# A linear-attention and Mamba kernel: two rows scanned by one instruction across neighbouring PSUM banks

## The chip, the cores and the metric

The kernel runs on one core of a Trainium2 chip. The time is the device time in microseconds of one execution; of three runs of the kernel before, the median is 8722.74 us (8712.8 to 8732.38 us). A core has five engines with instruction queues of their own: PE (TensorE, matrix products), DVE (VectorE), ACT (ScalarE), POOL (GpSimd) and SP (SyncE, which here issues the transfers). They run side by side and meet only at semaphores. PSUM is the small memory that PE writes its products to; DVE and ACT can read and write it too[...]. It has eight banks of 512 fp32 values in each of the 128 partitions.

## The reference, cut to what matters

The input x is (8, 512, 48, 48): 8 samples, 512 channels, 2304 places. Two layers follow, each behind a group norm and with a residual around it. The first is causal linear attention with eight heads. The second splits the channels into four groups of 128; each group, one after the other, goes through a Mamba block, and its fused output is added to the next group's input. The heart of a Mamba block is a recurrence over the places, for 256 channels times 16 states:

```python
q = einsum('nchw,oc->nohw', gn(x), Wq); k, v = ...        # layer 0
out = x + num(q, k, v) / den(q, k)
...
delta = softplus(dt @ Wdt.T + bdt)                         # layer 1, a Mamba block
A = -exp(A_log)
dA = exp(einsum('bld,dn->bldn', delta, A))
dBu = einsum('bld,bln->bldn', delta * xs, Bm)
def step(h, inp):
    dA_t, dBu_t, C_t = inp
    h = dA_t * h + dBu_t
    return (h, einsum('bdn,bn->bd', h, C_t))
_, ys = scan(step, h0, (dA, dBu, Cm))
y = (ys + xs * D) * silu(z)
out = y @ Wo.T
```

## The kernel before, in words

**Tiling.** The 2304 places are cut into six chunks of LC = 384. A job is one chunk of one Mamba block: 8 samples x 4 blocks x 6 chunks are 192 jobs. The 256 x 16 recurrences of a job fill 128 partitions 32 times. They are worked off in eight slots of four rows, a row being one recurrence on 128 partitions over the 384 places; a slot's index is k, and 192 x 8 = 1536 slots follow one another. Two streams of jobs (even and odd samples) take turns.

**A slot.** A tile `u` of [128, 2, 2, 1 + 384] holds the four rows. Column 0 of each row is the state at the end of the chunk before. `last_product` (L849) copies it there on ACT (L855), unless the job is the first chunk of its block (`self.c` is 0), and has POOL write the last 128 columns of delta * xs * B (L856); `product` (L864) has DVE write the other 256 (L867). `decay` (L873) has ACT write exp(delta * A) of one row into one PSUM bank (L877). `scan` (L885) has DVE run the recurrence of one row in place in `u` with the decays of that bank (L888). Column 0 of the decay is exp(0), so that the scan's first step, with initial value 0, takes over the state as it stands; the zeros for it are kept in column 0 of `drs` (L120). In a first chunk the scan is 384 long and column 0 is left out. `weigh` (L898) then has POOL multiply the whole of `u` by C (L900), `keep` (L907) has ACT save the last column as the state (L911), and `gather` (L913) has PE sum the rows into the tile `yp` (L916), which has a PSUM bank of its own.

**The banks.** Six PSUM banks, six separate tiles `bank0` to `bank5` (L126), are shared by everything else: the decays; the conv, gate and small projections of the Mamba blocks (`prepare`, L681); their output projection (L934); and the whole attention (`chunk`, L273) with its products on PE, its evictions on ACT and DVE, and one ACT instruction that works in place in a bank (the Relu at L306). `take` hands out a free bank, the list `spare` holds the free ones, and `Banks` is what the tasks use to take and free them.

**The order.** The schedule is the order in which the Python code emits instructions; each engine's queue has its instructions in that order. The framework adds the waits: an instruction that writes a tile waits until the earlier reads and writes of that tile by other engines are done, and one that reads a tile waits for the earlier writes of it.

`slot(k)` (L1137) emits one slot: the product of slot k+1, the tasks that are due (`beside`), the four scans with `ahead(DEPTH)` after each, and in the middle the rest of the tasks and the POOL product of slot k+2. `ahead(n)` (L1103) emits decays until n of them stand ready and unscanned; with DEPTH = 3 ACT is up to three rows ahead of DVE. A task is a Python generator that yields when it wants to go on and how many free banks it needs; `fits` (L987) holds it back while there are fewer.

Of the kernel before, what the change touches and what calls it, by code (L numbers as in the profile page):

```python
# [9 lines left out]
F32 = mybir.dt.float32  # L10
BF16 = mybir.dt.bfloat16
AF = mybir.ActivationFunctionType
ALU = mybir.AluOpType
# [4 lines left out]
P = 128  # L18
T = 128
LC = 384  # L20
NG = 2
SLOTS = 8
TAIL = 128
BANKS = 6
DEPTH = 3
LEAD = 11
ALONE = 4

# [22 lines left out]
def attention_then_mamba_kernel(  # L51
# [17 lines left out]
    nc = tc.nc  # L69
# [5 lines left out]
    cpool = ctx.enter_context(tc.tile_pool(name="consts", bufs=1))  # L75
# [5 lines left out]
    ps1 = ctx.enter_context(tc.tile_pool(name="ps1", bufs=1, space=PSUM))  # L81
# [35 lines left out]
    for t in dbcs:  # L117
        nc.gpsimd.memset(t[32:64, :], 1.0)

    drs = [cpool.tile([P, 2, 1 + LC], F32, name=f"dr_{i}") for i in range(2)]  # L120
    for t in drs:
        nc.gpsimd.memset(t[:, :, 0:1], 0.0)

    spare = [ps1.tile([P, 512], F32, name=f"bank{i}") for i in range(BANKS)]  # L126
    hot = []

    def take(decay=False):
        first = [b for b in spare if (b.name in hot) == decay]  # L130
        b = (first or spare)[0]
        spare.remove(b)
        if b.name in hot:
            hot.remove(b.name)
        return b

    class Banks:
# [4 lines left out]

        def __call__(self):
            self.held.append(take())
            return self.held[-1]

        def free(self, n=1, late=False):
            for _ in range(n):
                b = self.held.pop(0)
                if late:  # L150
                    hot.append(b.name)
                spare.append(b)


# [9 lines left out]
    def flush(every=True):  # L164
        while stores and (every or stores[0][0] <= half_no[0] - 2):
            _, o, i = stores.pop(0)
            nc.sync.dma_start(out=o, in_=i)
# [506 lines left out]
    class Job:  # L674
# [6 lines left out]
        def prepare(self):  # L681

            st, c = self.stream, self.c
            n = self.n = f"{st.n}_{c}"
# [3 lines left out]
            bank = Banks()  # L688
# [28 lines left out]
            first = 2 * self.start  # L717
# [9 lines left out]
            ]  # L727
            ahead(DEPTH + 2)
            nc.scalar.activation(xs[:, 0, :], xc0, AF.Silu, bias=pv[:, 0:1])  # L729
# [31 lines left out]
            delta = mpool.tile([P, 2, LC], F32, tag="delta", name=f"delta_{n}", bufs=1)  # L761
            ahead(DEPTH + 2)
            for h in range(2):
# [7 lines left out]
            def spread(what):  # L771
                s = dpool.tile([256, LC], F32, tag="dscr", name=f"{what}_{n}", bufs=6)
                nc.sync.dma_start(out=s.rearrange("(h p) l -> p h l", h=2), in_=delta)
                return s.rearrange("(h g d) l -> h d g l", h=2, g=2)

            dsrc = spread("dscr")
# [5 lines left out]
            def pairs(t, rows):  # L782
                for i in range(2):
                    nc.sync.dma_start(out=t[i * 64 : i * 64 + 64], in_=rows)

            def steps(h):
                self.dr[h] = drs[h]
                pairs(self.dr[h][:, :, 1 : 1 + LC], dsrc[h])

            def scaled(h):  # L790
                self.dxr[h] = mpool.tile([P, 2, LC], F32, tag="dxr", name=f"dxr_{n}_{h}")
# [57 lines left out]
        def last_product(self, s):  # L849

            shape, cols = [P, NG, 2, TAIL], slice(LC - TAIL, LC)
            u = mpool.tile([P, NG, 2, 1 + LC], F32, tag="u", name=f"u_{self.n}_{s}", bufs=5)
            if self.c:
                h, q = s // 4, s % 4 * NG
                nc.scalar.copy(u[:, :, :, 0], self.state[:, h, q : q + NG, :])  # L855
            nc.gpsimd.tensor_tensor(  # L856
                u[:, :, :, 1 + LC - TAIL :],
                self.B[s % 4][:, :, cols].unsqueeze(2).to_broadcast(shape),
                self.dxr[s // 4][:, :, cols].unsqueeze(1).to_broadcast(shape),
                ALU.mult,  # L860
            )
            return u
# [7 lines left out]
                self.dxp.unsqueeze(1).to_broadcast(shape),  # L870
            )

        def decay(self, s, i):  # L873
            h, q, j, g = s // 4, s % 4 * NG, i // 2, i % 2
            dA = take(decay=True)
            cols = slice(0 if self.c else 1, 1 + LC)
            nc.scalar.activation(  # L877
                dA[:, cols],
                self.dr[h][:, g, cols],
                AF.Exp,  # L880
                scale=self.w[6][:, 2 * h + g, q + j : q + j + 1],
            )
            return dA

        def scan(self, s, i, u, dA):  # L885
            j, g = i // 2, i % 2
            cols = slice(0 if self.c else 1, 1 + LC)
            nc.vector.tensor_tensor_scan(  # L888
                u[:, j, g, cols],
                dA[:, cols],  # L890
                u[:, j, g, cols],
                0.0,
                ALU.mult,
                ALU.add,
            )
            spare.append(dA)

        def weigh(self, s, u):  # L898

# [74 lines left out]
    slots = SLOTS * len(jobs)  # L974
# [31 lines left out]
    tasks, heads = [], []  # L1006
# [13 lines left out]
    def finale(job):  # L1020
        yield "0", 1
        job.project()
        yield "1", 0
        job.maximum()
        if job.c == NC - 1:
            yield from job.stream.pass_on()
# [4 lines left out]
    for b in counted:  # L1031
        first = times[parts.index((b, 0, 0))]
# [19 lines left out]
    def prune():  # L1052
        tasks[:] = [t for t in tasks if t.need is not None]
        heads[:] = [t for t in heads if t.need is not None]

    def beside(half):

        half_no[0] = half
        flush(every=False)
        begin(half // 2 + LEAD)  # L1060

        for t in heads:
            if t.need is not None and t.need[1] == 0 and t.fits() and t.due():
                t.step()
        held = False
        for t in tasks + heads:
            while t.need is not None and t.due():
                if not t.fits() or held and t.need[1]:
                    held = held or t.need[1] > len(spare)
                    break  # L1070
                t.step()
        prune()
# [19 lines left out]
    def at(k):  # L1092
        return jobs[k // SLOTS], k % SLOTS

    def apart(k):

        return k % SLOTS == 0 and k > 0 and at(k)[0].c == 0 and at(k)[0].stream is at(k - 1)[0].stream

    us, decays, waiting, kept = {}, [], [], []
    todo = 0  # L1100
    primed, drawn = set(), set()

    def ahead(n):  # L1103

        nonlocal todo
        while len(decays) < n and spare and todo < 4 * slots:
            k = todo // 4
            if apart(k) and k not in primed:
                break
            job, s = at(k)  # L1110
            if not job.prepared or s // 4 not in job.dr:
                break
            decays.append(job.decay(s, todo % 4))
            todo += 1

    def close(k):

# [9 lines left out]
    def prime(k):  # L1127
# [6 lines left out]
        job.product(s, us[k])  # L1134
        ahead(DEPTH)

    def slot(k):  # L1137
        job, s = at(k)
        end = k + 1 == slots or apart(k + 1)
        if not end and k + 1 not in drawn:  # L1140
            j, r = at(k + 1)
            j.product(r, us[k + 1])
        before = jobs[k // SLOTS - 1] if k >= SLOTS else None
        if s == 2 and before is not None and not before.closed:
            before.gated(1)
            tasks.insert(0, Task(finale(before)))
        elif s == 6:
            job.gated(0)
        beside(2 * k)
        for i in range(4):  # L1150
            job.scan(s, i, us[k], decays.pop(0))
            if i == 0 and s in (2, 6):
                job.skip(s // 4)
            ahead(DEPTH)
            if i == 1:

                while kept:
                    kept.pop(0)()
                if len(waiting) > 1:
                    waiting.pop(0)()  # L1160
                if s == 2:
                    job.inputs(1)
                elif s == 6 and k + 2 < slots and not apart(k + 2):
                    j = at(k + 2)[0]
                    if not j.prepared:
                        hurry(k + 2, lambda: j.prepared)
                    j.inputs(0)
                if not end and k + 2 < slots and not apart(k + 2):
                    j, r = at(k + 2)
                    us[k + 2] = j.last_product(r)  # L1170
                    if s == 7:

                        j.product(r, us[k + 2])
                        drawn.add(k + 2)
                beside(2 * k + 1)
        u = us[k]
        job.weigh(s, u)
        kept.append(lambda: at(k)[0].keep(s, u))
        waiting.append(lambda: at(k)[0].gather(s, us.pop(k)))
        if end:  # L1180
            close(k)
            if k + 1 < slots:
                prime(k + 1)
            else:
                hurry(slots, lambda: not tasks)
                flush()
# [82 lines left out]
```

## Time and profile before

| What | us |
|---|---|
| median of 3 runs | 8722.74 |
| the profiled execution | 8723.09 |
| its span, first to last instruction | 8721.0 |
| DVE busy | 8072.2 |
| POOL busy | 7834.3 |
| PE busy | 7774.7 |
| ACT busy | 6852.0 |
| of DVE: the scans (L888), 6144 of them | 5455.4 |
| of ACT: the decays (L877), 6144 of them | 3405.1 |
| of PE: the gathering into `yp` (L916) | 2417.7 |

The span divided by the 1536 slots is 5.68 us a slot. Busy time is the time in which an engine had an instruction running; four engines are busy for 79 to 93 per cent of the span, so most of the work lies side by side. In the profile's lists of instructions "x2" behind a name stands for two of them in a row, merged into one line, and the time ahead of the engine's name is that from the first one's start to the last one's end. The granted TensorE clock (PEclk, 1 is full speed) was 0.964 on average.

### The profile page before, as it was taken

Reading aid. Unit: us, or ns where it says so; the run is one execution under the profiler, and the core shown is the slowest. Engines: PE = TensorE matmul, PEld = TensorE weight load, DVE = VectorE, ACT = ScalarE, POOL = GpSimd, SP = SyncE. Lnnn points to the kernel's source line nnn. Section 1 sums busy time; section 2 is a strip of 40 time slices with the busy share of each in tenths; the row PEclk is TensorE's granted clock in tenths of the full one; section 3 lists DMA queues with packets and bytes.
Section 4 is the critical chain, followed back from the end, with each engine's and each line's share of the span. In section 5 each row is a group of like instructions: output and inputs, shape, how many; then the busy total and the mean of one; then the engine's idle time right before and its main releaser. Section 6 shows DMA issues by size and latency. Waiting matters only on the chain. (4 is left out here: it accounts for less than half of the span.)

```text
span 8721.0 us, 124881 instructions
## 1 busy us (share of the span) xinstructions
PE 7774.7 (89%) x36482; PEld 3714.5 (43%) x36482; DVE 8072.2 (93%) x11078; ACT 6852.0 (79%) x14500; POOL 7834.3 (90%) x4343
## 2 busy tenths in 40 slices
PE   7899999988899999998889999999889999999965
PEld 4444444444444444444444444444444444444422
DVE  2899999999899999998899999999889999999998
ACT  2788888777788888877778888887777888888876
POOL 1789999999999999998998999998999889999998
PEclk9999999999999999999999999999999999999987
DMA  5667777776766777776676777776666667766665
GB/s 183 168 178 190 196 198 197 191 191 189 195 188 190 193 200 199 197 189 191 187 193 186 193 190 197 196 197 187 188 185 194 188 188 190 189 188 185 183 165 146
DMA packets 1002924, 1643.11 MB, mean 188 GB/s; under 512 B 138592, under 2 KB 797312, under 8 KB 1002240
## 3 DMA queue, kind: packets, MB, share of 16 engines
q1 hardware_dynamic: 1002240, 1635.13, 69.1%
q8 instruction: 290, 4.75, 0.2%
q14 instruction: 394, 3.23, 0.1%
HBM read 1309.06 MB, written 325.58 MB: 187 GB/s over the span
## 5 line engine op out<-in xcount | busy, mean ns | idle before, releaser
L888 DVE TENSOR_TENSOR_SCAN u<-bank,u 128x385 f32<-128x385 f32 (+1 forms) x6144 | 5455.4, 938 | 327.4 <-ACT bank L877 288.3
L900 POOL TENSOR_TENSOR u<-u,C 128x1536 f32<-128x1536 f32 x1536 | 4892.7, 3185 | 345.6 <-DVE u L888 186.9
L877 ACT ACTIVATE bank<-dr,av 128x385 f32<-128x385 f32 (+1 forms) x6144 | 3405.1, 578 | 671.0 <-DVE u L888 575.2
L916 PE MATMUL yp<-u,cst 128*64 128x384 f32 x12288 | 2417.7, 515 | 343.9 <-POOL u L900 259.6
L856 POOL TENSOR_TENSOR u<-B,dxr 128x512 f32<-128x512 f32 x1536 | 1969.9, 1283 | 17.5 <-DMA dxr<-xscr 15.4
L867 DVE TENSOR_TENSOR u<-B,dxp 128x1024 f32<-128x1024 f32 x1536 | 1835.0, 1195 | 9.7 <-ACT dxp L840 9.7
L293 PE MATMUL bank<-xn,wq_sb 128*128 128x384 f32 x4608 | 1725.8, 519 | 74.2 <-DVE u L888 33.0
L916 PEld LDWEIGHTS yp<-u,cst 128*64 128x64 f32 x12288 | 780.7, 139 | 1557.9 <-issue 871.9
L693 PE MATMUL bank<-xi,wk 128*128 128x384 f32 x3072 | 1110.7, 505 | 198.6 <-ACT kl L390 108.7
L293 PEld LDWEIGHTS bank<-xn,wq_sb 128*128 128x128 f32 x4608 | 867.4, 199 | 842.4 <-DVE u L888 140.0
L693 PEld LDWEIGHTS bank<-xi,wk 128*128 128x128 f32 x3072 | 558.8, 192 | 761.4 <-ACT kl L390 211.6
L805 POOL TENSOR_TENSOR delta<-delta,xs 128x384 f32<-128x384 f32 x384 | 385.7, 1005 | 361.8 <-DMA dscr<-delta 234.6
L305 ACT ACTIVATE ex<-bank,bqkv_sb 128x384 f32<-128x384 f32 x384 | 221.5, 577 | 505.3 <-PE bank L293 505.3
L877 ACT ACT_TABLE_LOAD x382 | 490.1, 1283 | 6.8
L845 ACT ACTIVATE yp<-xs,pv 128x384 f32<-128x384 f32 x384 | 223.6, 582 | 278.0 <-DVE yz L928 277.5
L934 PE MATMUL bank<-yz,wo 128*128 128x384 f32 x768 | 302.1, 510 | 24.4 <-DVE yz L928 17.3
L753 PE MATMUL bank<-dbc,wd 9*128 9x384 f32 x768 | 312.4, 527 | 3.7 <-ACT dbc L745 3.7
L704 PE MATMUL bank<-xi,wi 128*128 128x384 f32 x768 | 287.5, 495 | 9.7 <-ACT xs L729 9.7
L423 PE MATMUL bank<-cst,rdb 128*128 128x128 f32 x576 | 110.0, 304 | 200.9 <-DVE u L888 198.7
L740 PE MATMUL bank<-xs,wx 128*40 128x384 f32 x768 | 280.0, 487 | 2.7 <-ACT sm L457 2.7
L476 PE MATMUL bank<-sm,v 128*64 128x128 f32 x2304 | 257.1, 302 | 0.0
L729 ACT ACT_TABLE_LOAD x192 | 246.3, 1283 | 3.6 <-PE bank L693 0.2
(117 smaller groups left out, 7978.0 us busy)
## 6 DMA issues: line engine op xcount, KB each, us to landing
B<-scr SPq DMA_DIRECT2D x1536, 192.0 KB
C<-scr SPq DMA_DIRECT2D x1536, 192.0 KB
xn<-xn SPq DMA_DIRECT2D x192, 768.0 KB
dr<-dscr SPq DMA_DIRECT2D x768, 192.0 KB
dxr<-xscr SPq DMA_DIRECT2D x768, 192.0 KB
dscr<-delta SPq DMA_DIRECT2D x192, 384.0 KB
xscr<-delta SPq DMA_DIRECT2D x192, 384.0 KB
xn<-in_x SPq DMA_DIRECT2D x48, 768.0 KB
```

What stands on the lines that cost most here:

```text
L293: nc.tensor.matmul(ps, wq_sb[:, kt, j * 512 + o * P : j * 512 + (o + 1) * P], xn[:, kt, :], start=(kt == 0), stop=(kt == 3),)
L693: nc.tensor.matmul(xc, wk[:, k, h * P : (h + 1) * P], xi[:, c0 + k : c0 + k + LC], start=(k == 0), stop=(k == 3),)
L704: nc.tensor.matmul(zp, wi[:, 256 + h * P : 256 + (h + 1) * P], xi[:, c0 + 3 : c0 + 3 + LC], start=True, stop=True,)
L753: nc.tensor.matmul(vp, wd[32:41, h * P : (h + 1) * P], dbc[32:41, :], start=True, stop=True)
L805: nc.gpsimd.tensor_tensor(delta[:, h, :], delta[:, h, :], xs[:, h, :], ALU.mult)
L856: nc.gpsimd.tensor_tensor(u[:, :, :, 1 + LC - TAIL :], self.B[s % 4][:, :, cols].unsqueeze(2).to_broadcast(shape), self.dxr[s // 4][:, :, ...
L867: nc.vector.tensor_mul(u[:, :, :, 1 : 1 + LC - TAIL], self.B[s % 4][:, :, cols].unsqueeze(2).to_broadcast(shape), self.dxp.unsqueeze(1).to ...
L877: nc.scalar.activation(dA[:, cols], self.dr[h][:, g, cols], AF.Exp, scale=self.w[6][:, 2 * h + g, q + j : q + j + 1],)
L888: nc.vector.tensor_tensor_scan(u[:, j, g, cols], dA[:, cols], u[:, j, g, cols], 0.0, ALU.mult, ALU.add,)
L900: nc.gpsimd.tensor_tensor(u[:, :, :, 0:LC], u[:, :, :, 1:], self.C[s % 4].unsqueeze(2).to_broadcast([P, NG, 2, LC]), ALU.mult,)
L916: nc.tensor.matmul(self.yp[g * 64 : g * 64 + 64, 0:LC], pair_sum, u[:, j, g, 0:LC], start=False, stop=(s % 4 == 3 and j == NG - 1), skip_g ...
L934: nc.tensor.matmul(self.xm[:, 0:LC], self.w[2][:, h, :], self.yz[:, h, :], start=(h == 0), stop=(h == 1),)
```

## The change

The six bank tiles become one tile, `banks`, of 6 x 512 columns, and a bank is now a number. In an even bank the decays of a row lie in the last 384 columns, in an odd one in columns 1 to 384, and the column in front of them is set to zero once, at the start (`front`). So the decays of two rows in an even bank and the odd one behind it, each with a zero ahead, are one stretch of 2 x 385 columns. Two neighbouring rows of `u`, each with its state in column 0, are a stretch of 2 x 385 as well, and one scan instruction runs over both: at the second row's column 0 the decay is 0, so that what came before is dropped and the state is taken over.

`take_two` looks for two such free banks, `decay` writes one row or two, and `scan` takes what `decay` left. `ahead` asks for two banks when the row isn't a slot's last one, and falls back on a single row only when fewer than SINGLE = 2 rows stand ready. Column 0 of `u` is now always written: with the state, or with the zeros of `rest` in a first chunk. `take` prefers a bank whose loss leaves the most couples whole. `room` emits decays ahead of the tasks if the due tasks' banks are left over. All other users of the banks get the 384 columns that their bank's decays have.

```diff
+SINGLE = 2
...
-    drs = [cpool.tile([P, 2, 1 + LC], F32, name=f"dr_{i}") for i in range(2)]
-    for t in drs:
-        nc.gpsimd.memset(t[:, :, 0:1], 0.0)
-    spare = [ps1.tile([P, 512], F32, name=f"bank{i}") for i in range(BANKS)]
-    hot = []
+    drs = [cpool.tile([P, 2, LC], F32, name=f"dr_{i}") for i in range(2)]
+    rest = cpool.tile([P, NG, 2], F32, name="rest")
+    nc.gpsimd.memset(rest, 0.0)
+    banks = ps1.tile([P, BANKS * 512], F32, name="banks")
+    spare, hot = list(range(BANKS)), []
+
+    def front(b):
+        return 512 * b + (511 - LC if b % 2 == 0 else 0)
+
+    for b in spare:
+        nc.vector.memset(banks[:, front(b) : front(b) + 1], 0.0)
...
+    def take_two():
+        twos = [b for b in spare if b % 2 == 0 and b + 1 in spare]
+        if not twos:
+            return None
+        def rank(b):
+            return -(b in hot) - (b + 1 in hot), max(spare.index(b), spare.index(b + 1))
+        b = min(twos, key=rank)
+        drop(b)
+        drop(b + 1)
         return b
...
         def __call__(self):
             self.held.append(take())
-            return self.held[-1]
+            first = 1 + front(self.held[-1])
+            return banks[:, first : first + LC]
...
-            if self.c:
-                h, q = s // 4, s % 4 * NG
-                nc.scalar.copy(u[:, :, :, 0], self.state[:, h, q : q + NG, :])
+            h, q = s // 4, s % 4 * NG
+            nc.scalar.copy(u[:, :, :, 0], self.state[:, h, q : q + NG, :] if self.c else rest)
...
-        def decay(self, s, i):
-            ...
+        def decay(self, s, i, first, n):
+            h, q = s // 4, s % 4 * NG
+            for r in range(n):
+                j, g = (i + r) // 2, (i + r) % 2
+                nc.scalar.activation(
+                    banks[:, 1 + front(first + r) : 1 + front(first + r) + LC],
+                    self.dr[h][:, g, :],
+                    AF.Exp,
+                    scale=self.w[6][:, 2 * h + g, q + j : q + j + 1],
+                )
+            return first, n
+
+        def scan(self, i, u, entry):
+            first, n = entry
+            size, at = n * (1 + LC), front(first)
+            rows = u.rearrange("p j g l -> p (j g l)")[:, i * (1 + LC) : i * (1 + LC) + size]
+            nc.vector.tensor_tensor_scan(
+                rows, banks[:, at : at + size], rows, 0.0, ALU.mult, ALU.add
             )
-            spare.append(dA)
+            spare.extend(range(first, first + n))
+            return n
...
     def ahead(n):
-        while len(decays) < n and spare and todo < 4 * slots:
-            k = todo // 4
+        while sum(e[1] for e in decays) < n and spare and todo < 4 * slots:
+            k, i = todo // 4, todo % 4
...
-            decays.append(job.decay(s, todo % 4))
-            todo += 1
+            first = take_two() if i < 3 else None
+            if first is None and sum(e[1] for e in decays) >= SINGLE:
+                break
+            two = first is not None
+            decays.append(job.decay(s, i, first if two else take(decay=True), 1 + two))
+            todo += 1 + two
+
+    def room():
+        need = sum(t.need[1] for t in tasks + heads if t.need is not None and t.due())
+        if len(spare) >= need + 2:
+            ahead(DEPTH)
...
+        room()
         beside(2 * k)
-        for i in range(4):
-            job.scan(s, i, us[k], decays.pop(0))
-            if i == 0 and s in (2, 6):
+        ahead(DEPTH)
+        i = 0
+        while i < 4:
+            was, i = i, i + job.scan(i, us[k], decays.pop(0))
+            if was == 0 and s in (2, 6):
                 job.skip(s // 4)
-            ahead(DEPTH)
-            if i == 1:
+            if was < 2 <= i:
...
+                room()
                 beside(2 * k + 1)
+            ahead(DEPTH)
```

More of the change, by code (lines that the diff above doesn't have):

```diff
@@ L118, in attention_then_mamba_kernel, with couples, drop @@
         nc.gpsimd.memset(t[32:64, :], 1.0)
-    drs = [cpool.tile([P, 2, 1 + LC], F32, name=f"dr_{i}") for i in range(2)]
-    for t in drs:
-        nc.gpsimd.memset(t[:, :, 0:1], 0.0)
-    spare = [ps1.tile([P, 512], F32, name=f"bank{i}") for i in range(BANKS)]
-    hot = []
-    def take(decay=False):
[L130 to L134, printed above, removed]
+    drs = [cpool.tile([P, 2, LC], F32, name=f"dr_{i}") for i in range(2)]
[7 more added lines that the diff above has]
+        nc.vector.memset(banks[:, front(b) : front(b) + 1], 0.0)
+    def couples(free):
+        return sum(b + 1 in free for b in free if b % 2 == 0)
+    def drop(b):
+        spare.remove(b)
+        if b in hot:
+            hot.remove(b)
+    def take(decay=False):
+        left = {b: couples([f for f in spare if f != b]) for b in spare}
+        b = min(spare, key=lambda b: ((b in hot) != decay, -left[b], spare.index(b)))
+        drop(b)
+        return b
+    def take_two():
[5 more added lines that the diff above has]
+        b = min(twos, key=rank)
+        drop(b)
+        drop(b + 1)
         return b
@@ L150, in free @@
                 if late:
-                    hot.append(b.name)
+                    hot.append(b)
                 spare.append(b)
@@ L787, in steps @@
                 self.dr[h] = drs[h]
-                pairs(self.dr[h][:, :, 1 : 1 + LC], dsrc[h])
+                pairs(self.dr[h], dsrc[h])
             def scaled(h):
@@ L871, in product @@
             )
-        def decay(self, s, i):
[L874 to L881, printed above, removed]
-            )
[L883 to L895, printed above, removed]
-            spare.append(dA)
+        def decay(self, s, i, first, n):
[15 more added lines that the diff above has]
+                rows, banks[:, at : at + size], rows, 0.0, ALU.mult, ALU.add
+            )
+            spare.extend(range(first, first + n))
+            return n
         def weigh(self, s, u):
```

## The prediction

> **What bounds the kernel now.** I read the busy shares first, then the costliest groups, the list of waits, and last the timeline, to see what lies beside what.
>
> ```profile
> PE 7774.7 (89%) x36482; PEld 3714.5 (43%) x36482; DVE 8072.2 (93%) x11078; ACT 6852.0 (79%) x14500; POOL 7834.3 (90%) x4343
> ...
> L888 DVE TENSOR_TENSOR_SCAN u<-bank,u 128x385 f32<-128x385 f32 (+1 forms) x6144 | 5455.4, 938 | 327.4 <-ACT bank L877 288.3
> L900 POOL TENSOR_TENSOR u<-u,C 128x1536 f32<-128x1536 f32 x1536 | 4892.7, 3185 | 345.6 <-DVE u L888 186.9
> L877 ACT ACTIVATE bank<-dr,av 128x385 f32<-128x385 f32 (+1 forms) x6144 | 3405.1, 578 | 671.0 <-DVE u L888 575.2
> ...
> L293 PE MATMUL bank<-xn,wq_sb 128*128 128x384 f32 x4608 | 1725.8, 519 | 74.2 <-DVE u L888 33.0
> ```
>
> Four engines are nearly full, DVE most of all, and two thirds of DVE is the scans. DVE is idle for 8721 - 8072 = 649 us, 288 of them because a decay is late:
>
> ```profile
> DVE u L888 <- ACT bank L877: 288.3, 213, 4.5
> ```
>
> That is 213 waits in 6144 scans: ACT is otherwise ahead. The time holds only because the users of the banks work at once, as the timeline shows (start, duration, engine, line):
>
> ```profile
> 4001.19 2.85 PE L293 MATMUL bank<-xn,wq_sb 128*128 128x384 f32 x8
> ...
> 4003.02 3.50 DVE L888 TENSOR_TENSOR_SCAN u<-bank,u 128x385 f32<-128x385 f32 x4
> ...
> 4003.34 0.85 ACT L457 ACTIVATE sm<-bank 128x384 f32<-128x384 f32 x2
> ...
> 4004.08 1.08 ACT L877 ACTIVATE bank<-dr,av 128x385 f32<-128x385 f32 x2
> ...
> 4005.41 0.91 PE L462 MATMUL bank<-xr,cst 128*128 128x384 f32 x2
> ```
>
> While DVE scans from 4003.02 to 4006.52, ACT writes two decays (4004.08) and PE a product (4005.41), each to another bank. The reader should keep these 3.5 us in mind. The last view is the end of the run, where PE has less to do:
>
> ```profile
> 8580.00:8700.00 120.00, 72.55 (x231) 24.67 (x232) 108.55 (x127) 75.51 (x165) 116.13 (x64) 0.70 0.49 134
> ```
>
> ```profile
> 8606.51 5.40 PE L693 MATMUL bank<-xi,wk 128*128 128x384 f32 x8 [1.27 <-POOL xi L667]
> ...
> 8613.27 2.85 PE L693 MATMUL bank<-xi,wk 128*128 128x384 f32 x8
> ```
>
> With PE busy for 72.55 of 120 us the granted clock was 0.70, and the same eight matmuls took 5.40 us once and 2.85 us 7 us later.
>
> **What the Trainium skill says.** (1) "VectorE: DVE Perf Modes", section "The DRAIN you can't avoid": each DVE operation empties its pipeline at the end, so the count of operations is to be kept small. The trace agrees: a scan alone is 0.938 us, but four in a row take 3.50, so (3.50 - 0.938) / 3 = 0.854 us apart. (2) "PSUM — Partial Sum Buffer", section "PSUM bank collisions raise a hardware error": two engines must be kept apart on one bank and quadrant, while accesses to different banks run clean. The overlap at 4003 to 4006 us agrees; the hardware doesn't ask for an order between banks. (3) "TensorE: Matmul & The Clock Gate", part 1: after an idle window of about 3.4 us PE's clock is halved until it has been busy for about as long. 5.40 against 2.85 us agrees.
>
> **The change part by part.**
>
> *Fewer scans.* In the changed program as built there are 3071 double scans and 2 single ones, so nearly every pair is joined. A double scan isn't in the trace. Below: the two forms of 385 and 384 elements last 939 and 937 ns, so 2 ns an element, 0.938 + 0.77 = 1.71 us. Above: 0.938 + 0.854 = 1.79, nothing saved. I take 1.74. In a row, two single scans cost 1.71 of DVE's time; a double one would save at most the 0.854 - 0.77 = 0.08 us between them, 3071 x 0.08 = 250 us. That is the whole of the gain there is. 256 more copies of a zero state (193 ns each on ACT, 49 us) and one column less in each decay (1 ns) are nothing beside it, covered by ACT's 21% idle time.
>
> *One tile in place of six.* This decides. The waits are laid tile by tile, and `banks` is now one tile. I read the built program's waits: a scan of banks 2 and 3 waits for the projection matmul that was emitted just ahead of it and writes bank 0, and for the decays of the next pair in banks 4 and 5; that matmul waits for the decays before it, and a decay waits for the scan and the matmuls before it, whatever bank they used. Followed through all waits, every write to `banks` comes after every earlier access to it by another engine, and every read after every earlier write, without exception. In the program of before, of 19,666 cases of a bank write and the latest earlier one of another engine, 17,700 had no order between them. Only reads can still lie beside reads.
>
> So the accesses to `banks` form a single file: 10,766 stretches, 2328 of PE writes, 3455 of ACT writes (3071 times a pair of decays, 384 times the Relu) and 4982 of reads (3071 with a scan), one single stretch of zeros aside. Between two scans there is now always a pair of decays, and on average 2328 / 3071 = 0.76 PE stretches. The file's length is a sum, with the durations of the page:
>
> - Scans: 3071 x 1.74 = 5345 us.
> - Pairs of decays: two take 1.09 us in the timeline, overlapping; the second now waits for the first, so 2 x 0.578 + 0.04 (the gap between L406 and L407, a wait on its own engine) = 1.20. 3071 x 1.20 = 3685. Lower bound 1.09: 3347.
> - PE's writes to banks: PE's busy time less the gathering into `yp`, which comes in 1536 lines of x8 with 1.51 us, 2319 us: 7775 - 2319 = 5456 at the clock of before.
> - The Relu in place, L306: 208.8 us, say 209.
> - DVE's evictions (L350, L358, L379, L428, L945: 520; L406, L407, L413, L415: 176), some tails overlapping: 650.
> - ACT's evictions: in 1911 stretches of reads there is no scan, and 2616 of the 3024 evictions stand in these. By line (L305 221, L457 160, L364, L729, L732 112 each, L733, L734 94, L390, L391 184, parts of L486, L745, L375, L764: 240) 1330, less the overlaps of neighbours: 1250.
> - Handing over: scan to decay 0.05 us (scan ending at 4001.13, PE starting 4001.18), PE to ACT 0.03 to 0.04. 10,766 x 0.05 = 540; bounds 0.04 to 0.08, 430 to 860.
> - What stands in the queue between two steps of the file: two table loads of 1.28 us around each Softplus that a scan of 1.74 hides in part, the state copies of 0.19 us ahead of an eviction. I put 400; none at best, 900 at worst.
> - Start and end without scans: 60.
>
> The sum is 17.6 ms with PE at its old clock. The products (L867, 1.195 us) stay hidden: each stands between two scans, where DVE waits 1.25 us for decays anyway. POOL (7834 us) and the transfers fall far below the file; cover is no question for them.
>
> *PE's clock.* In the file PE waits for scan, decays and evictions, 1.74 + 1.20 + 0.5 us and the hand-overs, some 3.6 us between its stretches of 5456 / 2328 = 2.3 us, with a gathering of 1.5 us in some of these gaps. It would be busy for under half of the time, less than in the last 120 us of the trace, where the clock was 0.70. Bounds: none slower (x1.0), nearly all at half (x1.75). I take x1.35 (a clock of 0.72 against 0.964): 5456 x 0.35 = 1910 us more, 19.5 ms; as the gaps are often just at the skill's 3.4 us and the gatherings break them up, I go down a little, to 19,200 us.
>
> **The rivals.**
>
> - *The file, but PE keeps its clock*: 17.6 ms. For it: gaps of 3 to 4 us near 8620 us didn't always slow PE. Against: 0.70 at the end.
> - *The file with PE cold nearly throughout*: 17.6 + 5456 x 0.75 = 21.7 ms. For it: bursts of 2.3 us are shorter than the warm-up.
> - *A file of scans and decays alone*, PE's products slipping in beside them: 3071 x (1.74 + 1.20 + 0.1) = 9.3 ms, with the evictions and a third of PE's writes about 13 ms. Against: PE's waits are in the program.
> - *The gain as the sum of DVE gives it, not slower*: the single mechanism is the saved gap between scans, deciding if the waits between different banks are long satisfied when they are reached. 8723 - 170 = 8550 us, taking 0.055 us for each of the 3071. For it: DVE is the fullest engine. Against: those waits name instructions emitted directly ahead, not old ones; from one decay pair in the file on, 3071 x 1.2 = 3.7 ms outweigh it.
>
> **How the numbers follow.** The file with a slower PE 0.63, full clock 0.17, cold 0.10, scans and decays alone 0.07, the gain 0.02, and 0.01 for no change. About 0.2% is what can be told from none. The range takes the main case with its bounds (decays 1.09, hand-overs, queue work: -0.9 to +0.8 ms; PE x1.15 to x1.55: 1.1 ms either way, not all at once), and half of the first two rivals: 17,000 to 21,400 us. The sum stands for a whole profiled execution, which before was 8723.09 us with a span of 8721.0, 0.4 us from the median; the difference is nothing here.
>
> **What would show it.** Right: scans of about 1.74 us x3073; DVE idle above 9 ms, waiting at the scan's line for PE and ACT; never a scan beside a decay in the timeline; all engines below half busy; PEclk at 0.65 to 0.85. Wrong: scans beside decays of other banks, DVE still above 85%. The point would be off if PEclk stayed at 0.95, or if a hand-over cost 0.1 us and more.

## The result, and the profile after

The changed kernel takes 21,664.15 us (median of four runs, 21,659.46 to 21,676.35), beside 8721.17 us of the kernel before on the same chip: a ratio of 2.484, 95% interval 2.480 to 2.488. The profiled execution has a span of 21,661.2 us, 14.1 us a slot. Forecast were 19,200 us and a range up to 21,400; the sign and the mechanism held in the main, the size did not. Three kernels below ran once: the kernel before with one tile, and the change with idle matmuls and with Relu.

First the page of the kernel after: busy time, share of the span and count of each engine; then the granted clock in 40 slices; then three of the costliest groups (line, engine, operation, shapes, count, then busy us and mean ns, then idle time ahead and what ended most of it).

```profile
PE 11938.5 (55%) x36482; PEld 5316.0 (25%) x36482; DVE 8233.5 (38%) x8013; ACT 7314.9 (34%) x14756; POOL 7846.8 (36%) x4342
...
PEclk7666666666666666666666666666666666666666
...
L913 DVE TENSOR_TENSOR_SCAN u<-banks,u 128x770 f32<-128x770 f32 (+1 forms) x3073 | 5405.1, 1759 | 12554.4 <-ACT banks L901 3060.6
...
L901 ACT ACTIVATE banks<-dr,av 128x384 f32<-128x384 f32 x6144 | 3592.4, 585 | 13121.8 <-DVE u L913 11586.4
...
L318 PE MATMUL banks<-xn,wq_sb 128*128 128x384 f32 x4608 | 2304.3, 662 | 66.2 <-DVE q L375 35.9
```

The work of DVE, ACT and POOL is what it was, within 7 per cent. The scans are joined and even take 50 us less in all (5405.1 against 5455.4). But DVE, full to 93% before, is now busy for 38%, and no engine is above 55%: they take turns. DVE waits 12,554 us ahead of its scans, against 327 before, and ACT 13,122 us ahead of its decays. PE's clock is at 0.6 to 0.7 after the first slice; L318, the projection that was L293, takes 662 ns a matmul, not 519.

The list of waits of DVE (who <- for whom: us, times, longest) says that it is not the scan's own decays alone that are late:

```profile
DVE u L913 <- ACT banks L901: 3060.6, 414, 12.3
DVE u L913 <- PE banks L318: 2543.7, 363, 9.6
DVE u L913 <- PE banks L501: 1223.2, 182, 9.7
DVE u L913 <- PE banks L729: 1156.4, 188, 7.9
```

No scan uses what L318, L501 or L729 (projection, attention output, gate) compute. They are waited for only because they write other banks of the same tile. The timeline shows the turns (start, duration, engine, line; in brackets idle time and what ended it):

```profile
10001.89 1.76 DVE L913 TENSOR_TENSOR_SCAN u<-banks,u 128x770 f32<-128x770 f32 x1 [3.03 <-PE banks L765]
10003.69 1.20 ACT L901 ACTIVATE banks<-dr,av 128x384 f32<-128x384 f32 x2 [4.73 <-DVE u L913]
...
10004.92 0.47 ACT L770 COPY dbc<-banks 40x384 f32<-40x384 f32 x1
...
10005.45 1.44 PE L423 MATMUL banks<-cst,pr 128*128 128x2 f32 x6 [3.66 <-ACT dbc L770]
...
10006.82 0.70 PE L428 MATMUL banks<-v,kl 128*64 128x64 f32 x8
...
10007.73 1.76 DVE L913 TENSOR_TENSOR_SCAN u<-banks,u 128x770 f32<-128x770 f32 x1 [4.07 <-POOL xn L342]
...
10009.52 1.20 ACT L901 ACTIVATE banks<-dr,av 128x384 f32<-128x384 f32 x2 [3.93 <-DVE u L913]
```

Each line that names `banks` begins 0.03 to 0.21 us after the one above it has ended, the second line of PE aside, which follows PE's own first one and overlaps it: the scan ends at 10003.65 and the decays start at 10003.69; these end at 10004.89, then an eviction runs, then PE, then the next scan. (At 10007.73 the list of releasers names POOL; the last access to a bank before it is PE's, ending at 10007.52.) In the timeline shown of before, ACT and PE wrote banks while DVE scanned.

From the trace the intervals of all instructions that touch a bank can be laid over each other. Before, 2136 us of decays and 3299 us of PE's bank writes lay beside a scan. After, the two overlaps are 0.0 us, and so is every other one between two engines. That holds for reads beside reads too: DVE's and ACT's accesses to the tile never overlap, so here a read of the tile waits not only for earlier writes of it, as was said of the framework above, but for earlier reads by other engines as well. So the span can be added up:

| us | forecast | measured |
|---|---|---|
| scans | 5345 | 5405 |
| decays | 3685 | 3592 |
| PE's writes to banks | 5456 x 1.35 = 7366 | 8409 |
| Relu in place | 209 | 210 |
| DVE's evictions | 650 | 662 |
| ACT's evictions | 1250 | 1453 |
| neighbours on one engine that overlap | in the rows above | -94 |
| no bank in use | 540 + 400 + 60 = 1000 | 2024 |
| sum | 19,505, put at 19,200 | 21,661 |

### The profile page after: what moved, and what is told of

The parts are those of the page before. It is cut to its first block, busy times and chain, and to the rows that moved or that the text cites. A ratio compares the mean times of both kernels' runs of the same rounds, so it can differ in the third digit from the quotient of the medians.

```text
span 21661.2 us, 123752 instructions
## 1 busy us (share of the span) xinstructions
PE 11938.5 (55%) x36482; PEld 5316.0 (25%) x36482; DVE 8233.5 (38%) x8013; ACT 7314.9 (34%) x14756; POOL 7846.8 (36%) x4342
## 5 line engine op out<-in xcount | busy, mean ns | idle before, releaser
L913 DVE TENSOR_TENSOR_SCAN u<-banks,u 128x770 f32<-128x770 f32 (+1 forms) x3073 | 5405.1, 1759 | 12554.4 <-ACT banks L901 3060.6
L901 ACT ACTIVATE banks<-dr,av 128x384 f32<-128x384 f32 x6144 | 3592.4, 585 | 13121.8 <-DVE u L913 11586.4
L937 PE MATMUL yp<-u,cst 128*64 128x384 f32 x12288 | 3707.1, 739 | 1692.8 <-ACT state L932 802.4
L318 PE MATMUL banks<-xn,wq_sb 128*128 128x384 f32 x4608 | 2304.3, 662 | 66.2 <-DVE q L375 35.9
L718 PE MATMUL banks<-xi,wk 128*128 128x384 f32 x3072 | 1492.0, 643 | 565.2 <-ACT before L400 134.0
L318 PEld LDWEIGHTS banks<-xn,wq_sb 128*128 128x128 f32 x4608 | 1203.3, 271 | 995.3 <-issue 716.2
L718 PEld LDWEIGHTS banks<-xi,wk 128*128 128x128 f32 x3072 | 750.2, 258 | 1485.5 <-issue 965.4
L765 PE MATMUL banks<-xs,wx 128*40 128x384 f32 x768 | 533.6, 850 | 837.9 <-ACT v L416 621.9
L729 PE MATMUL banks<-xi,wi 128*128 128x384 f32 x768 | 468.5, 702 | 929.8 <-ACT xs L754 929.8
L778 PE MATMUL banks<-dbc,wd 9*128 9x384 f32 x768 | 503.7, 801 | 480.4 <-DVE S L440 257.1
L955 PE MATMUL banks<-yz,wo 128*128 128x384 f32 x768 | 471.9, 759 | 21.8 <-ACT banks L901 13.6
```

Of the source, the lines that this page charges most:

```text
L318: nc.tensor.matmul(ps, wq_sb[:, kt, j * 512 + o * P : j * 512 + (o + 1) * P], xn[:, kt, :], start=(kt == 0), stop=(kt == 3),)
L718: nc.tensor.matmul(xc, wk[:, k, h * P : (h + 1) * P], xi[:, c0 + k : c0 + k + LC], start=(k == 0), stop=(k == 3),)
L729: nc.tensor.matmul(zp, wi[:, 256 + h * P : 256 + (h + 1) * P], xi[:, c0 + 3 : c0 + 3 + LC], start=True, stop=True,)
L765: nc.tensor.matmul(dps[0:40, 0:LC], wx[:, h, :], xs[:, h, :], start=(h == 0), stop=(h == 1))
L778: nc.tensor.matmul(vp, wd[32:41, h * P : (h + 1) * P], dbc[32:41, :], start=True, stop=True)
L901: nc.scalar.activation(banks[:, 1 + front(first + r) : 1 + front(first + r) + LC], self.dr[h][:, g, :], AF.Exp, scale=self.w[6][:, 2 * h + ...
```

## The experiments

**The tile alone, put into the kernel before.** Six slices of one tile; scans, order and choice of banks as they were.

```diff
-    spare = [ps1.tile([P, 512], F32, name=f"bank{i}") for i in range(BANKS)]
+    banks = ps1.tile([P, BANKS * 512], F32, name="banks")
+    spare = list(range(BANKS))
...
-            return self.held[-1]
+            return banks[:, 512 * self.held[-1] : 512 * self.held[-1] + 512]
...
```

> The kernel before with the six banks as slices of one tile, everything else as before: single scans, no zeros, the old order. Theory A: a single file again, with single scans and single decays: 6144 scans of 0.938 (5763 us against 5405) and 6144 more hand-overs of 0.05, so as slow as the change or a little slower, 21,500 to 23,000 us. Theory B: the scans are single, so 8,700 to 9,500 us.

It took 22,576 us, with DVE waiting at its scans as in the changed kernel:

```profile
L889 DVE TENSOR_TENSOR_SCAN u<-banks,u 128x385 f32<-128x385 f32 (+1 forms) x6144 | 5865.3, 957 | 13146.2 <-PE banks L294 2692.6
```

The merging of the tiles alone costs more than the whole change, with no double scan in the program. Theory B is out. The 6144 single scans are busy for 5865 us, the joined ones of the changed kernel for 5405: in a single file, joining takes up to 460 us off the scans.

**The change without the one tile.** Three tiles of two banks, the least that a double scan needs; and six tiles with two single scans in place of a double one.

```diff
-    banks = ps1.tile([P, BANKS * 512], F32, name="banks")
+    couple = [ps1.tile([P, 1024], F32, name=f"couple{i}") for i in range(BANKS // 2)]
```

> The change as it is, but with three tiles of two banks each in place of one tile of six; the double scans stay. Theory A (one tile makes every access to any bank wait for all earlier ones): only accesses within a couple still queue up, so nearly all of the 12.9 ms goes: 8,500 to 9,300 us, scans beside decays again, TensorE's clock at 0.93 or more. Theory B (the joined scan itself, which wants two decays and two neighbouring free banks at once, starves VectorE): nothing of that is changed, so above 15,000 us.

```diff
...
-            size, at = n * (1 + LC), front(first)
-            rows = u.rearrange("p j g l -> p (j g l)")[:, i * (1 + LC) : i * (1 + LC) + size]
-            nc.vector.tensor_tensor_scan(
-                rows, banks[:, at : at + size], rows, 0.0, ALU.mult, ALU.add
-            )
+            for r in range(n):
+                at = front(first + r)
+                rows = u[:, (i + r) // 2, (i + r) % 2, :]
+                nc.vector.tensor_tensor_scan(
+                    rows, tiles[first + r][:, at : at + 1 + LC], rows, 0.0, ALU.mult, ALU.add
+                )
```

> The change's order, its couples of banks and its kept zeros, but six tiles of one bank and two single scans in place of each double one. Theory A: no wait between banks, so near the kernel before: 8,650 to 8,950 us; what it is above 8,722 is the price of handing out banks in couples, and what e1 is below it is the worth of a joined scan (250 us at most). Theory B, if it is the couples and not the joined instruction: above 12,000 us.

They took 11,160 us (ratio 1.281, 1.278 to 1.284) and 9633 us (1.106, 1.103 to 1.108). So 10.5 of the 12.9 ms go with three tiles and 12.0 with six: theory A in the main. Decays lie beside scans again, for 1572 us with three tiles and 2063 with six (0.0 in the changed kernel, 2136 before). But both times lie above what was expected, and something else costs 0.9 ms. The waits of DVE in the three-tile kernel show a part of what is left there:

```profile
DVE fg L969 <- ACT couple L334: 797.3, 178, 6.4
```

The eviction `fg` of a Mamba output waits for the Relu of an attention projection that stands in the other half of its couple: the false wait in small.

**The joined scan by itself.** The three tiles of two banks, with two single scans.

```diff
-            nc.vector.tensor_tensor_scan(
-                rows, span(first, at, size), rows, 0.0, ALU.mult, ALU.add
-            )
+            for r in range(n):
+                rows = u[:, (i + r) // 2, (i + r) % 2, :]
+                dA = span(first + r, front(first + r), 1 + LC)
+                nc.vector.tensor_tensor_scan(rows, dA, rows, 0.0, ALU.mult, ALU.add)
```

> e1_couples (three tiles of two banks) with two single scans in place of each double one; order, banks and waits between a couple's halves as in e1. It prices the joined scan by itself. If a joined scan saves 0.05 to 0.08 us and VectorE's queue is what ends things: 11,250 to 11,450 us. If waiting for both decays before the first row can start costs more than that: below 11,100 us, at the lowest towards e3's 9,633.

11,086 us (1.271, 1.269 to 1.274): 74 us faster than with joined scans, though DVE's scans are busy for 5464.4 us and not 5318.4. The 146 us of DVE that joining saves are real but shorten nothing there. That joining makes it slower in all is what the second case of the expectation said; the reason (the second row's decay must be ready for the first row to start, and both banks stay taken until the end) is argued, not shown.

**Where the 0.9 ms come from.** In the six-tile kernel, three things are left of the change: which bank is chosen, decays by twos, and where they are emitted; and the kept zeros. The first was undone in e5, the second too in e9; the zeros were put alone into the kernel before.

```diff
-        left = {b: couples([f for f in spare if f != b]) for b in spare}
-        b = min(spare, key=lambda b: ((b in hot) != decay, -left[b], spare.index(b)))
+        first = [b for b in spare if (b in hot) == decay]
+        b = (first or spare)[0]
...
-        twos = [b for b in spare if b % 2 == 0 and b + 1 in spare]
-        if not twos:
+        if len(spare) < 2:
             return None
...
+        return take(decay=True), take(decay=True)
```

> The six tiles and two single scans of e3_six_tiles, with the change's order of emission, but a bank is chosen as before: the one that came free longest ago, and two decays take any two free banks. Theory D (what e3 lost, 910 us, is the choice of banks: keeping couples whole hands a task the bank freed last, so TensorE waits for its eviction): 8,700 to 8,950 us. Theory E (the order of emission, decays by twos and only when two banks are free, is what costs): 9,400 us or more.

```diff
-            first = take_two() if i < 3 else None
-            if first is None and sum(e[1] for e in decays) >= SINGLE:
-                break
+            first = None
```

> e5_oldest with decays emitted one by one whenever a bank is free, as before, instead of by twos; where in the slot they are emitted stays as in the change (after the due tasks, not straight after the scan in the slot's middle). If it is the twos that cost: 8,700 to 8,950 us. If it is the places of emission: 9,300 us or more.

> The kernel before with the kept zeros alone: a zero in column 0 of each of the six bank tiles, decays of 384 columns behind it, column 0 of u always written, scans always 385 long; tiles, order and choice of banks as before. Predicted as nothing (256 more copies of 0.19 us on ScalarE, which is idle 21 per cent of the time; 1024 scans one column longer, 2 us in all): 8,690 to 8,760 us. If the added copies or the shifted columns matter: above 8,780 us.

The choice of banks gives back 146 us (9488 us, ratio 1.088, 1.086 to 1.090), the twos another 788 us: decays one by one take 8700 us (median of six runs; 0.9972 of before, 0.9960 to 0.9984). The zeros alone take 8725 us (1.0004, 0.9995 to 1.0013), as forecast nothing. So it is the twos, not the places of emission. (The second edit also drops the rule that holds single decays back once two rows stand ready; the twos and this rule were not parted.) In the order of emission four rows stand decayed at 2672 of the 6144 scans with twos and at 190 without, and four rows are four of six banks; that the tasks then wait for banks fits, but was not tried by itself. With twos DVE waits most for an attention product and for a Relu of the attention, the first two lines, and less for its decays, the third. Without them the wait for decays, the last line, is the only one above 80 us:

```profile
DVE rd L424 <- PE bank L421: 276.0, 134, 13.8
DVE k L376 <- ACT bank L324: 243.7, 185, 3.1
DVE u L907 <- ACT bank L894: 172.6, 159, 5.0
```

```profile
DVE u L907 <- ACT bank L894: 261.7, 210, 4.4
```

**Fewer couples.** The third couple split into two lone banks, without and with single decays whenever no couple is free (SINGLE = 4).

```diff
-    couple = [ps1.tile([P, 1024], F32, name=f"couple{i}") for i in range(BANKS // 2)]
+    couple = [ps1.tile([P, 1024], F32, name=f"couple{i}") for i in range(2)]
+    lone = [ps1.tile([P, 512], F32, name=f"bank{i}") for i in (4, 5)]
```

> e1_couples with the third couple split into two tiles of one bank: two couples for double scans, two lone banks that tasks take first. Theory A (waits between banks that share a tile are what remains in e1): between e3 and e1, 9,800 to 10,600 us. If the couples as such (two neighbours must be free) cost: above 11,160 us, since there are fewer of them.

> e7_split with SINGLE = 4: a single decay is emitted whenever no couple is free, so that 1530 scans are single and 2307 double. Theory E (decays held back until two neighbours are free): faster than e7_split by 200 us or more. Theory D (the choice of banks): within 150 us of e7_split.

The split gives 10,313 us (1.183, 1.181 to 1.185), 847 us less than three couples, as waits within shared tiles would have it. SINGLE = 4 gives 11,110 us (1.274, 1.271 to 1.276), slower by 797 us, which neither theory expected. The lists of waits show where it comes from; the largest new entry is this:

```profile
DVE u L920 <- PE couple L418: 1101.9, 148, 8.5
```

Single decays now take lone banks and halves of couples, and more of PE's products land in couples: 5239 of its matmuls, against 2498 without SINGLE = 4. Scans wait for such products, which they don't use, for 1590 us in all, against 5. So this too is the false wait between the halves of a shared tile.

**PE's clock.** Six idle matmuls behind each scan in PE's order, in unused columns of `yp`'s bank.

```diff
+    def idle_work(n):
+        for _ in range(n):
+            nc.tensor.matmul(
+                yp[:, LC:512], ident, cst[:, 0:P], start=False, stop=True, skip_group_check=True
+            )
...
             was, i = i, i + job.scan(i, us[k], decays.pop(0))
+            idle_work(6)
```

> The change with six more matmuls of 128 columns on TensorE behind each scan in its order, into 128 unused columns of yp's bank, to keep TensorE from standing idle; the rest as it is. Theory A with a slowed clock as a follower: TensorE's clock goes from 0.68 to 0.85 or more, its writes to banks from about 8.4 ms towards 5.5 ms, and the time to 18,500 to 20,000 us. Theory C (the low clock is the main cause): below 14,000 us. If the clock has no part in it: 21,600 us or more, for the added work.

20,971 us: a gain of 693, less than expected, although the clock rose to 0.828. The account of its trace says why: PE's writes fall from 8409 to 7312 us, and the time without a bank in use grows from 2024 to 2429, as the idle matmuls sometimes stand in the way: they run during 327 us of the longer of these gaps (0.3 us and more). The sum of the two, -1097 + 405 = -692, is the gain. And PE's writes did not get the mean clock. Weighted with the time in which PE wrote banks, the clock was 0.723 there and 0.623 in the changed kernel (means over the whole span 0.828 and 0.681):

| kernel | clock while PE writes banks | 0.970 / clock | PE's bank writes, us | over before's 5539 |
|---|---|---|---|---|
| before | 0.970 | 1 | 5539 | 1 |
| six tiles, by twos | 0.924 | 1.05 | 5832 | 1.05 |
| three couples | 0.866 | 1.12 | 6160 | 1.11 |
| the change, idle matmuls | 0.723 | 1.34 | 7312 | 1.32 |
| the change | 0.623 | 1.56 | 8409 | 1.52 |

(5539 us is laid out from the intervals, as the column is; the prediction's 5456 is the busy time less the gatherings.) So by this sum the clock carries about 2.9 of the 12.9 ms, as a follower of the file: theory C is out. No run had the file and the old clock together, so the 2.9 ms are worked out and not measured. The traces record the granted clock in steps of 3.41 us. In the changed kernel PE stands idle for 3.4 us or longer 1528 times, before 41 times.

**What stands in ACT's queue.** Relu in place of Silu and Softplus.

```diff
...
-                nc.scalar.activation(delta[:, h, :], vps[h], AF.Softplus)
+                nc.scalar.activation(delta[:, h, :], vps[h], AF.Relu)
```

> The change with Relu in place of Silu and Softplus in the Mamba blocks, so that ScalarE loads no tables between (the output is another function). Theory F (in a single file ScalarE comes to a table load only when it is its turn, so nothing hides it; 741 us of the 982 us of loads lie where no bank is in use): 20,700 to 21,100 us. Rival (they lie beside the waits of other engines and cost nothing, as the prediction's 400 us for all queue work supposed): 21,400 us or more.

20,807 us, 857 less: theory F. The time without a bank in use goes from 2024 to 1257 us, which is 767 of the 857; most of the rest is in PE's writes to banks, 8320 us in place of 8409. In the timeline of the changed kernel the wait is plain:

```profile
10016.43 1.20 ACT L901 ACTIVATE banks<-dr,av 128x384 f32<-128x384 f32 x2 [5.71 <-DVE u L913]
...
10018.08 1.28 ACT L789 ACT_TABLE_LOAD   x1
10019.37 0.87 ACT L789 ACTIVATE delta<-banks 128x384 f32<-128x384 f32 x2
...
10020.35 1.76 DVE L913 TENSOR_TENSOR_SCAN u<-banks,u 128x770 f32<-128x770 f32 x1 [2.90 <-ACT u L879]
```

The decays are done at 10017.63, but the scan starts at 10020.35, after the load and the Softplus evictions, the second of which ends at 10020.24: these only read other banks, and even a read waits for a read. (The view names the state copy L879, the last on ACT to end before the scan starts. But that copy writes the `u` of two slots later, and DVE's wait for ACT ends in the trace at 10020.30, before the copy does at 10020.33.)

## Why the prediction was right in kind and wrong in size

- *One tile makes a single file.* Right, and shown from both sides: the tile alone makes the kernel before slow (22,576 us), and taking the one tile from the change gives back 10.5 to 12.0 of 12.9 ms.
- *PE's clock, x1.35.* The term that failed most: 8409 us, x1.54, 1043 us more than its 7366. The step took a mean clock, 0.72, close to the 0.70 of the trace's end, for the clock during the work. Even the right mean, 0.681, would have given only 0.964 / 0.681 = 1.42. PE was at half clock in 75 per cent of the time in which it wrote banks and in 56 per cent of the rest, so the work saw 0.623. Going down from 19.5 to 19.2 ms because the gaps were taken to be often just at 3.4 us went the wrong way: 1528 gaps lasted that long or longer.
- *Handing over and queue work, 1000 us.* The other term that failed, 2024 us. The hand-overs themselves were near: the gaps below 0.3 us make 768 us, 577 of them between two engines (8345 gaps, 0.069 each), where 540 for 10,766 had been put; most of the others lie between two decays of a pair and were forecast with these. The longer gaps, start and end included, make 1256 us, where 400 and 60 had been put. Two things had been left out. The forecast counted the table loads around each Softplus and took them to be hidden in part; there are as many around the Silus, 768 in all. The gaps ahead of ACT's lines that load tables (L754, L789, L901) make 835 us, and 55 without the loads. The gaps ahead of PE's lines L718 and L955 make another 325 us, and in 322 of these PE is at gatherings, which stand ahead in its queue.
- *Only reads can lie beside reads.* Wrong. Every read waits for earlier reads too, so ACT's evictions are in the file whole, 1453 us and not 1250, and a Softplus holds up a scan that could have run beside it.
- *Scans 5345, decays 3685, Relu 209, DVE's evictions 650.* Right within 3 per cent. A double scan takes 1.759 us; 1.74 had been taken between 1.71 and 1.79.
- *The gain of joined scans, 250 us at most.* Right as a bound on what DVE is spared beside the kernel before: 50 us less busy time in the changed kernel, 146 us between the two three-tile kernels, and none of it reaches the end. Of the 84 ns put between two scans, joining saved 33 to 48.
- *The change of order, not costed at all.* Wrong, though hidden under the file: decays by twos cost 788 us and the choice of banks 146 us once the tiles are apart.
- *Products, kept zeros, POOL and transfers hidden.* Right: POOL is busy for 36%, and the zeros cost nothing (1.0004).

The rivals: the file with a cold PE throughout, 21.7 ms at 0.10, came nearest. PE wasn't cold throughout (0.623, not half), so it was right by its sum rather than by its account.

The fastest version is six tiles, two-row code and kept zeros, but single scans and decays one by one: 8700 us against 8722, 0.3 per cent, with an interval (0.9960 to 0.9984) that leaves out 1. Nothing of the joined scan is in it.

## What to carry to other kernels

Tiles are the grain of the waits. Merging buffers into one tile so that one instruction can span two of them puts every user of any of them in line; look at the waits of the built program before counting the saved overhead. A resource handed out by twos can have a price even without false waits. And when engines begin to take turns, what hid behind another engine (table loads, evictions, PE's products and their slowed clock) has to be paid for, nearly all of it.

## What the runs showed of the hardware

- The clock that PE's work gets can lie below the span's mean: 0.623 against 0.681 in the changed kernel, 0.723 against 0.828 with idle matmuls. Over five kernels the time of PE's bank writes went as the inverse of the former within 3 per cent.
- A scan over 770 columns across two PSUM banks takes 1759 ns, 821 more than one over 385 (938), while two single scans in a row are 854 apart: so joining two saved 938 + 854 - 1759 = 33 ns. By the two three-tile kernels it is (5464.4 - 5318.4) / 3071 = 0.048 us, or 48 ns.
- A table load of ACT takes 1.28 us. In the kernel before, 132 us of the 985 us of loads fell into times in which no bank was in use; in the changed kernel, where the engines take turns, 743 us did.
